# Two of four graph layers computed over lists of edges instead of over the full mask

## The chip, the cores and the metric

The kernel runs on one core of one Trainium2 chip. The metric is the time of one execution in device microseconds (us), first to last instruction of that core. Engines are named as in the profile: PE is the matrix engine and PEld its weight loads, DVE the vector engine, ACT the scalar engine, POOL GpSimd, SP the engine whose queue issues most DMAs.

## The reference, cut to what matters

The input `x` is 16 batches of 1024 nodes with 256 features; `adj` is one symmetric 1024x1024 mask for all of them. Four layers follow one another, each of the form `x = x + attention(relu(layernorm(x)))`:

```python
# layers 0 and 3: 4 heads of 64 features     (layer 1: the same with 1 head of 256)
Wh = (h @ W).reshape(B, N, 4, 64)
e  = s_src[:, :, None, :] + s_dst[:, None, :, :]        # one score per (query, neighbour, head)
e  = leaky_relu(e, 0.2);  e = where(adj, e, -inf)
out = elu(einsum('bijh,bjhd->bihd', softmax(e, axis=2), Wh))
# layer 2: e = (h W1)(h W2)^T, same mask and softmax, values h W3, relu
```

The mask is the same in every batch and layer. With this case's data it has 9052 ones among 1,048,576 places: 8.8 neighbours a query on the mean, 19 at most, at most 7 within any 128 neighbours in a row. Of 32 queries in a row the neighbours number 255 to 316.

## The kernel before, in words

`fast` (the other function, `general`, runs only where a check on the inputs fails) writes its whole program out through a planner. `Plan.add` takes a step: its engine, an assumed cost, a due time, the steps it waits for, and the buffers that it takes and gives back (`bufs`, by tag). `Plan.order` plays the steps through with those costs, always the ready step with the earliest due time on each engine, and the instructions are emitted in that order. Each engine then runs its own list strictly in that order on the chip. Layers of different batches are thereby woven into one another: constants such as `PERIOD`, `START`, `LEAD`, `LATER` say at which multiple of a period each (batch, layer) is due.

Nothing is gathered: every layer works on all 1024x1024 pairs of a batch, in two halves of 512 queries and 8 tiles of 128 neighbours. Scores of layers 0, 1, 3 factor, so that a weight is `max(row[query], ke[neighbour]) * mask`.

- `Layer.prologue` normalises (statistics by DVE at L831/L832, `rstd` by POOL's `pow` at L867, `h` by ACT at L901), transposes `h` with DMAs (L928, from SP), projects (`projected`, PE), and evicts the values into `val`, each head with one more column for the denominator (L982 to L993). The query factors are turned by PE (`er`), written to DRAM (L1062) and read back spread over 128 partitions (`row`, L1075, 256 KB each).
- `steps_a` serves layers 0 and 3. For each half, head and neighbour tile, 64 steps a layer: one DVE instruction writes a 128x512 tile `p` of weights (`weigh`, L1128), then PE multiplies it in (`attend`: for each of 4 query tiles `product` with 65 columns of `val`, gathered in a PSUM tile `acc`). Afterwards `invert` (L1161), `divide` (L1172 on DVE or L1175 on ACT), `elu` (L1094 to L1108) and, after layer 3, the store (L1199).
- `steps_b` serves layers 1 and 2, with `accb` as accumulator: 64 products a query tile, 257 columns wide. Layer 2 also computes its scores on PE (`pp<-qT,hT`).

`product` (L584) splits the stationary operand into two tiles of 64 columns which write to the two halves of the partitions; each call of `matmul` on f32 stands in the trace as two MATMULs and two LDWEIGHTS. So a layer 0 or 3 has 64 steps x 4 query tiles x 2 = 512 calls.

The order of DMAs on SP is that of the list too: a `row` load whose buffer isn't free holds up the transposes behind it.

Of the kernel before, what the change touches and what calls it, by code (L numbers as in the profile page):

```python
# [9 lines left out]
F32 = mybir.dt.float32  # L10
BF16 = mybir.dt.bfloat16
I32 = mybir.dt.int32
U16 = mybir.dt.uint16
# [36 lines left out]


PERIOD, EARLY = 190.0, 0.8711
START = {0: 0.0, 1: 1.0292, 2: 2.3297, 3: 3.7503}
LEAD = {0: 0.5727, 1: 0.718, 2: 0.2478, 3: 2.1041}
STEP = {0: 0.0094, 1: 0.0707, 2: 0.069, 3: 0.055}
WHEN = {
    (1, "weights"): ((-0.4736, 0.0028), (-0.1245, 0.0433)),
    (1, "attended"): ((0.7291, 0.0065), (0.2632, 0.174)),
    (2, "weights"): ((-0.1558, 0.0082), (0.3907, 0.0165)),
    (2, "attended"): ((0.6931, 0.1127), (0.5021, 0.0038)),  # L60
# [7 lines left out]
}  # L68
AHEAD = {
# [11 lines left out]
class Plan:  # L81
# [9 lines left out]
    def __init__(self, free, strict):  # L91
        self.free, self.steps, self.wide = dict(free), [], set()
        self.queues = {tag: [] for tag in strict}

    def add(self, engine, cost, due, fn, after=(), take=(), give=(), wide=False):
        s = len(self.steps)
        if wide:
            self.wide.add(s)
        self.steps.append([engine, cost, due, fn, tuple(a for a in after if a is not None), take, give])
        for tag in set(take) & set(self.queues):  # L100
            self.queues[tag].append(s)
        return s

    def order(self):
# [13 lines left out]
        self.starts = {}  # L118
# [10 lines left out]
        while True:  # L129
            again = True  # L130
            while again:
                again = False
                for engine, queue in ready.items():
# [19 lines left out]
                    k = pick[1]  # L153
                    for tag in steps[k][5]:
                        free[tag] -= 1
# [11 lines left out]
            if what == 0:  # L167
                idle[steps[k][0]] = True
            else:
                for tag in steps[k][6]:  # L170
                    free[tag] += 1
# [7 lines left out]
        return [steps[k][3] for k in res]  # L179
# [362 lines left out]
def fast(  # L542
# [26 lines left out]
    plan = Plan(bufs, ("p", "p1", "acc", "accb", "val4", "val1", "x", "row4", "row1"))  # L569
# [4 lines left out]
    dram = ctx.enter_context(tc.tile_pool(name="dram", bufs=4, space=DRAM))  # L574
    psum = ctx.enter_context(tc.tile_pool(name="psum", bufs=1, space=PSUM))

    def buf(tag, shape, dtype=F32, name=None):
        pool = psum if tag in ("pp", "acc", "accb") else sb
        return pool.tile(shape, dtype, name=name or tag, tag=tag, bufs=bufs[tag])
# [35 lines left out]
    faults = const.tile([P, 2], F32, name="faults")  # L615
    fine = const.tile([1, 1], F32, name="fine")
    x_tiles, mean_var, early = {}, {}, []
# [12 lines left out]
    def load_x(b, due, after=()):  # L630

        res = []
        for n, (t0, t1) in enumerate(PARTS[b == 0]):
# [3 lines left out]
            def fn(its=slice(t0, t1), apart=apart):  # L637
                if its.start == 0:
                    x_tiles[b] = buf("x", [P, NT, F], name="xt")
                (nc.scalar if apart else nc.sync).dma_start(  # L640
                    out=x_tiles[b][:, its, :], in_=x[b].rearrange("(t p) f -> p t f", p=P)[:, its, :]
                )

            s = plan.add(ACT if apart else SP, 0.5, due, fn, after, take=() if t0 else ("x",))
            after = () if b == 0 else (s,)
            res += [landed(s, due, 128 * (t1 - t0))] * (t1 - t0)
# [82 lines left out]
    def mask_steps():  # L729
        done = {}  # L730
        for n, (half, jh) in enumerate(((0, 0), (0, 1), (1, 0), (1, 1))):
            due, quarter = 15.0 + n if half else -1.5 if jh else SOON - 5.2, {}

            def load(half=half, jh=jh, quarter=quarter):
                raw = quarter["raw"] = buf("x", [P, HT, HALF], I32, name="raw")
                rows = adj[half * HALF : (half + 1) * HALF, jh * HALF : (jh + 1) * HALF]
                nc.sync.dma_start(out=raw, in_=rows.rearrange("(t p) j -> p t j", p=P))


            loaded = landed(plan.add(SP, 0.9, due, load, (first_x[2 if n == 0 else -1],), take=("x",)), due, 1024)  # L740
            for t in range(HT):
                tiles = {}

                def positive(t=t, tiles=tiles, quarter=quarter):
                    tiles["pos"] = sb.tile([P, HALF], BF16, name="pos", tag="h", bufs=bufs["h"])
                    nc.vector.tensor_scalar(tiles["pos"], quarter["raw"][:, t, :], 0.0, None, op0=OP.is_gt)

                s = plan.add(DVE, 0.36, due, positive, (loaded,), take=("h",), give=("x",) if t == HT - 1 else ())
# [8 lines left out]
                def keep(tiles=tiles, half=half, jh=jh, t=t):  # L757
                    copy = nc.scalar.copy if half else nc.vector.tensor_copy
                    copy(mask[half][jh][:, :, t * P : (t + 1) * P], tiles["tp"])

                s = plan.add(*((ACT, 0.6) if half else (DVE, 0.65)), due, keep, (s,), give=("pp",))
# [12 lines left out]
    def w12_steps(due):  # L774
# [28 lines left out]
        for fc in range(KC):  # L803
# [12 lines left out]
            s = plan.add(PE, 0.9, due, multiply, tuple(last), take=("pp",), give=("p1",), wide=True)  # L816
# [7 lines left out]
    def statistics(b, t, due, after):  # L824


        def fn():
            if b not in mean_var:
                mean_var[b] = small.tile([P, NT, 2], F32, name="mv", bufs=6)
            st = small.tile([P, 6], F32, name="bn")  # L830
            nc.vector.bn_stats(st, x_tiles[b][:, t, :])  # L831
# [5 lines left out]
    class Layer:  # L837
        def __init__(self, b, layer):
            self.b, self.layer = b, layer
            self.heads, self.gat = LAYERS[layer]  # L840
            self.closed = []

            self.filling = layer == 0 or layer == 3 and b >= B - 2

        def prologue(self, due, step, stats, direct=False):
# [7 lines left out]
            tag = f"val{heads}"  # L853
            T = {}
# [3 lines left out]
            for n, its in enumerate(slice(*part) for part in parts):  # L858

                def norm(its=its, n=n):  # L860
                    if n == 0:
                        T["rstd"] = small.tile([P, NT], F32, name="rstd")
                        T["shift"] = small.tile([P, NT], F32, name="nshift")
# [5 lines left out]
                def norm3(its=its, n=n):  # L869
# [7 lines left out]
                    self.val = buf(tag, [P, NT, heads, d + 1], name="val")  # L877
                    if self.gat:
                        ke = self.factors = small.tile([P, COLS], F32, name="ke", tag=f"ke{heads}", bufs=2)
# [3 lines left out]
                    else:  # L883
                        nc.gpsimd.memset(self.val[:, :, :, d : d + 1], 1.0)
                        self.hT = sb.tile([P, KC, N], F32, name="hT")
                        self.qT = sb.tile([P, KC, N], F32, name="qT")
# [4 lines left out]
                take = () if n else (tag,) if self.gat else (tag, "hq")  # L891
# [3 lines left out]
            for n, t0 in enumerate(range(0, NT, 2)):  # L895
                at = due + n * step

                def normed(t0=t0):
                    for t in (t0, t0 + 1):
# [3 lines left out]
                            x_tiles[b][:, t, :],  # L903
# [5 lines left out]
                s = plan.add(ACT, 1.05, at, normed, (ready[t0],), take=("h", "h"))  # L909
# [45 lines left out]
                for k in range(2):  # L955
                    t = t0 + k

                    def projected(t=t, t0=t0, k=k):
                        pv = T["pv", t] = buf("pp", [P, HALF])
# [9 lines left out]
                    s2 = plan.add(  # L969
                        PE, 0.9, at + (k + 1) * step / 3, projected, (s, w_ready), take=("pp",),  # L970
# [3 lines left out]
                    def evict(t=t, many=heads > 1 and (direct or not self.filling)):  # L974
                        to = self.val[:, t, :, :d]
# [4 lines left out]
                        a = self.val[:, t, :, d : d + 1]  # L980
# [4 lines left out]
                        nc.scalar.activation(self.ke[:, :, t], T["pv", t][:, F:cols], AF.Exp)  # L985
# [3 lines left out]
                    def scaled(t=t):  # L989
                        to = self.val[:, t, :, :d]  # L990
                        of = T["pv", t][:, :F].rearrange("p (h d) -> p h d", h=heads)
                        a = self.val[:, t, :, d : d + 1]
# [4 lines left out]
                    s2 = plan.add(ACT, cost, at, evict, (s2,), give=() if many else ("pp",))  # L997
# [3 lines left out]
                    evicted.append(s2)  # L1001
            at = due + 4 * step
            self.ready, self.queries = evicted, ([], [])
            if not self.gat:
                for dc in range(KC):
                    for n0 in range(0, N, HALF):

                        def query(dc=dc, n0=n0):
                            pq = T["pq", dc, n0] = buf("pp", [P, HALF])
# [9 lines left out]
                        s = plan.add(PE, 1.72, at, query, (*copies, *w12_ready), take=("pp",))  # L1019

                        def keep(dc=dc, n0=n0):
                            nc.scalar.copy(self.qT[:, dc, n0 : n0 + HALF], T["pq", dc, n0])
# [3 lines left out]
            self.rows, self.row_ready = {}, {}  # L1026

            if direct:
                for half in range(2):
                    for hd in range(heads):  # L1030

                        def spread(half=half, hd=hd):
# [453 lines left out]
```

## Time and profile before

| | |
|---|---|
| runs before | 2969.36 and 2970.18 us, median 2969.77 |
| profiled execution: span | 2969.3 us |
| PE busy | 2915.6 us, 98% |
| DVE busy | 2644.8 us, 89% |
| ACT busy | 1920.6 us, 65% |
| POOL busy | 227.0 us, 8% |
| DMA | 188.06 MB, mean 63 GB/s |
| granted PE clock, mean | 0.996 |

The table is read row against row: the time of an engine can't be less than its busy time, and only PE's comes near the span. "Busy" on PE is the union of overlapping instructions, so a group's busy time divided by its number of calls is the pace at which calls leave, while "mean ns" is the duration of a single one.

### The profile page before, as it was taken

How to read it: one execution, taken by the hardware profiler on the slowest of the kernel's cores; microseconds unless marked ns; L12 is line 12 of the kernel's file. 1: busy time of each engine (PE TensorE's matmuls, PEld its weight loads, DVE VectorE, ACT ScalarE, POOL GpSimd, SP SyncE). 2: the span in 40 equal slices, each digit the busy share in tenths (PEclk: the TensorE clock that was granted, in tenths of full speed). 3: DMA queues.
4: the chain of work that ended last, by engine and by line, in shares of the span. 5: the costliest groups of instructions: out<-in, count | busy, mean ns of one | idle time of the engine just before them, and what ended most of it. 6: DMA issues, size and time to landing. Idle time of an engine off the chain costs nothing.

```text
span 2969.3 us, 108633 instructions
## 1 busy us (share of the span) xinstructions
PE 2915.6 (98%) x47954; PEld 2296.6 (77%) x47954; DVE 2644.8 (89%) x5284; ACT 1920.6 (65%) x4776; POOL 227.0 (8%) x153
## 2 busy tenths in 40 slices
PE   8799999999999999999999999999999999999997
PEld 6687968778787786777787777887977779787876
DVE  8998988789989898998989989889999989687788
ACT  6785776876665767565775656766675575664633
POOL 2110100100100001010000100001001000000000
PEclk9999999999999999999999999999999999999999
DMA  4331323323122342322323213231332333120310
GB/s 144 71 86 39 67 51 94 74 60 81 42 59 66 66 80 52 79 46 56 77 70 78 45 50 73 66 69 47 71 75 51 63 76 70 34 59 23 63 34 25
DMA packets 344048, 188.06 MB, mean 63 GB/s; under 512 B 268880, under 2 KB 304400, under 8 KB 343568
## 3 DMA queue, kind: packets, MB, share of 16 engines
q1 hardware_dynamic: 342880, 180.25, 26.9%
q8 instruction: 378, 6.19, 0.9%
q14 instruction: 102, 0.84, 0.1%
q10 hardware_dynamic: 688, 0.79, 0.1%
HBM read 98.63 MB, written 17.33 MB: 39 GB/s over the span
## 4 chain that ended last, share of the span: by engine, by line
PE 85%; DVE 11%; ACT 2%; issue 1%; DMA 0%; POOL 0%; DVEq 0%; POOLq 0%
PE pp L584 30%; PE acc L584 27%; PE accb L584 27%; DVE p L1128 6%; DVE o L1099 1%; DVE bn L831 1%; DVE p L1252 0%; DVE p L1251 0%; DVE mv L832 0%; DMA turned<-planes 0%; DVE xt L1101 0%; ACT hTp L942 0%; ACT h L901 0%; DVE p L1219 0%; ACT planes L924 0%
## 5 line engine op out<-in xcount | busy, mean ns | idle before, releaser
L1128 DVE SCALAR_TENSOR_TENSOR p<-row,ke,mask 128x512 f32<-128x512 f32 x2048 | 1456.9, 766 | 63.5 <-PE acc L584 62.7
L584 PEld LDWEIGHTS acc<-val,p 128*64 128x64 f32 x32768 | 1066.3, 139 | 112.2 <-DVE p L1128 37.1
L584 PE MATMUL acc<-val,p 128*64 128x65 f32 x32768 | 1072.6, 223 | 29.9 <-DVE p L1128 28.6
L584 PE MATMUL accb<-val,p 128*64 128x257 f32 x8192 | 925.8, 380 | 0.1
L584 PEld LDWEIGHTS accb<-val,p 128*64 128x64 f32 x8192 | 703.3, 137 | 163.1 <-issue 5.1
L584 PE MATMUL pp<-qT,hT 128*64 128x512 f32 x2048 | 462.1, 593 | 0.2 <-ACT val L982 0.2
L584 PE MATMUL pp<-w,hTp 128*64 128x264 f32 (+1 forms) x3072 | 385.3, 388 | 4.8 <-ACT hTp L942 4.8
L584 PEld LDWEIGHTS pp<-qT,hT 128*64 128x64 f32 x2048 | 176.5, 137 | 208.2 <-issue 203.1
L584 PEld LDWEIGHTS pp<-w,hTp 128*64 128x64 f32 x3072 | 248.8, 138 | 87.9 <-issue 18.3
L901 ACT ACTIVATE h<-xt,nshift,rstd 128x256 f32<-128x256 f32 x512 | 275.1, 597 | 57.1 <-DVE nshift L870 56.5
L1286 ACT ACTIVATE o<-accb,rdens 128x256 f32<-128x256 f32 x128 | 60.7, 474 | 345.7 <-DVE rdens L1278 333.5
L924 ACT COPY planes<-h 128x512 uint16<-128x512 uint16 x496 | 281.2, 621 | 3.3 <-DMA turned<-planes 3.3
L1251 DVE SCALAR_TENSOR_TENSOR p<-u,p 128x512 f32<-128x512 f32 x256 | 174.9, 683 | 74.0 <-ACT p L1247 73.7
L867 POOL TENSOR_TENSOR rstd<-rstd,neg_half 128x8 f32<-128x8 f32 (+2 forms) x67 | 120.2, 1794 | 1425.6 <-DVE rstd L864 1029.0
L1246 ACT ACTIVATE u<-pp 128x512 f32<-128x512 f32 x256 | 153.0, 598 | 109.7 <-PE pp L584 100.5
L1175 ACT ACTIVATE o<-acc,rden 128x64 f32<-128x64 f32 x572 | 131.9, 317 | 140.7 <-DVE rden L1161 118.1
L831 DVE BATCH_NORM_STATS2 bn<-xt 128x6 f32<-128x256 f32 x512 | 212.0, 414 | 11.2 <-DMA xt<-in_x_dram 3.3
L942 ACT COPY hTp<-turned 128x1024 uint16<-128x1024 uint16 x184 | 214.0, 1167 | 6.8 <-DMA turned<-planes 6.7
L1252 DVE TENSOR_TENSOR p<-p,mask 128x512 f32<-128x512 f32 x256 | 177.1, 692 | 8.8
L1219 DVE SCALAR_TENSOR_TENSOR p<-row,ke,mask 128x512 f32<-128x512 f32 x256 | 182.1, 748 | 0.0
L987 ACT ACTIVATE val<-pp,val 128x64 f32<-128x64 f32 (+1 forms) x640 | 179.4, 347 | 0.0
L1247 ACT ACTIVATE p<-pp,shift_col 128x512 f32<-128x512 f32 x256 | 176.0, 687 | 0.0
(87 smaller groups left out, 1839.0 us busy)
## 6 DMA issues: line engine op xcount, KB each, us to landing
row<-er_d SPq DMA_DIRECT2D x272, 256.0 KB
xt<-in_x_dram SPq DMA_DIRECT2D x31, 512.0 KB
out_dram<-xt SPq DMA_DIRECT2D x31, 512.0 KB
raw<-in_adj_dram SPq DMA_DIRECT2D x4, 1024.0 KB
raw<-in_adj_dram SPq DMA_DIRECT2D x16, 256.0 KB
turned<-planes SPq DMA_TRANSPOSE x248
w<-in_L_gnn_W_dram SPq DMA_DIRECT2D x2, 256.0 KB
wraw<-in_L_gnn_W_dram SPq DMA_DIRECT2D x2, 256.0 KB
```

Of the source, the lines that this page charges most:

```text
L584: nc.tensor.matmul(to[c : c + COLS], stationary[:, c : c + COLS], moving, start=start, stop=stop, skip_group_check=True,)
L831: nc.vector.bn_stats(st, x_tiles[b][:, t, :])
L901: nc.scalar.activation(h, x_tiles[b][:, t, :], AF.Relu, bias=T["shift"][:, t : t + 1], scale=T["rstd"][:, t : t + 1],)
L924: nc.scalar.copy(to[:, :, :, k, :], of)
L942: nc.scalar.copy(bits, T["tp", t0].rearrange("p s c q -> p c q s"))
L987: nc.scalar.mul(to[:, hd, :], of[:, hd, :], a[:, hd, :])
L1128: nc.vector.scalar_tensor_tensor(p, lay.rows[half, hd], lay.ke[:, lay.heads + hd, jt : jt + 1], mask_of(half, jt), op0=OP.max, op1=OP.mult)
L1219: nc.vector.scalar_tensor_tensor(p, lay.rows[half, 0], lay.ke[:, 1, jt : jt + 1], mask_of(half, jt), op0=OP.max, op1=OP.mult)
L1246: nc.scalar.activation(u, e, AF.Exp, scale=1.0 - SLOPE)
L1247: nc.scalar.activation(p, e, AF.Exp, bias=shift_col, scale=SLOPE)
L1251: nc.vector.scalar_tensor_tensor(p, u, 1.0, p, op0=OP.max, op1=OP.mult)
L1252: nc.vector.tensor_mul(p, p, mask_of(half, jt))
```

## The change

Of the 32 (batch, layer) pairs of layers 0 and 3, all but (0, 0) and (15, 3) leave `steps_a`. They are joined in 15 slots of two. A slot's members share one table in DRAM and one stream of gathers:

```python
GROUP, TILES, MOST_OF = 32, 3, 24
WIDTH = 264
SLOTS = (((1, 0), (2, 0)), ((3, 0), (0, 3)), ((4, 0), (5, 0)),
         *(((b, 0), (b - 5, 3)) for b in range(6, 16)),
         ((11, 3), (12, 3)), ((13, 3), (14, 3)))
```

**Lists, once** (`edge_steps`, due early). For each group of 32 queries the neighbours are listed, padded to 3 tiles of 128 places: 32 groups x 3 = 96 lists. Eight loads of 512 KB bring the mask; for each, DVE runs a 128x1024 multiply, eight `max` over 128 columns (eight largest each), three `max` over 64 and two `match_replace`; then ranks, one-hot matrices and products choose what stands at each place. Left behind are `edge_of` (row numbers, 4096 and more at empty places), `pick` (which query of 32 an edge belongs to, 0 or 1) and its transpose `picked`. POOL clears the gather buffers once. A third check joins the two that decide whether `general` must run (a query with 24 neighbours, a group with over 384, or 8 within 128).

**Prologue of a member.** The values, 4x65 columns, and the neighbours' factors, 4 columns, make up a row of 264 f32 that goes to the table (`store`, SP, 264 KB for two tiles). The query factors aren't read back as `row`: DVE writes them in three bf16 parts, PE multiplies them by `picked` into one factor per edge (24 products of 128x48 a member, bf16), DVE adds the parts (`rs`).

**The slot** (`steps_c`), 24 units of four lists:

```python
        for u in range(UNITS):                      # UNITS = 8 query tiles x 3
            for g in range(NG):                     # NG = 4 groups of 32 queries
                nc.gpsimd.indirect_dma_start(
                    out=T["vg", u][:, g, :], out_offset=None, in_=slot.table[:, :],
                    in_offset=bass.IndirectOffsetOnAxis(ap=edge_of[:, u * NG + g : u * NG + g + 1], axis=0),
                    bounds_check=N - 1, oob_is_err=False,
                )
...
                nc.vector.tensor_tensor(w, slot.rs[...], vg[:, :, :, heads * (d + 1) :], OP.max)
                nc.vector.tensor_tensor(p, pick[:, u, :]..., w..., OP.mult)
...
                for m in range(many):               # two members
                    for hd in range(heads):
                        for g in range(NG):
                            nc.tensor.matmul(
                                acc[g * GROUP : (g + 1) * GROUP, hd, :],
                                p[:, m * heads + hd, g * GROUP : (g + 1) * GROUP],
                                vg[:, g, lo : lo + d + 1],
                                start=kt == 0 and hd == 0, stop=kt == TILES - 1, skip_group_check=True,
                            )
```

A gather fetches 128 rows of 528 f32 (2112 bytes) by the row numbers. `w` has 32 elements a partition, `p` 1024. The stationary tiles are 32 columns wide and write to four quarters of the partitions.

**Close of a query tile** (`closing`): reciprocal and one multiply of 128x256 on DVE, `elu` for two tiles at once. POOL's additions (L1108) and ACT's divisions and multiplications for these layers go to DVE.

**Buffers and queues.** `bufs` is cut anew; `Plan.homes` names each buffer by number:

```diff
-        "x": 5, "val4": 2, "val1": 2, "hq": 1, "row4": 3, "row1": 2, "h": 4, "planes": 2, "turned": 2, "hTp": 2, "p": 8, "p1": 18,
-        "u": 2, "o": 1, "ex4": 1, "o1": 2, "ex1": 2, "pp": 4, "acc": 2, "accb": 2,
+        "x": 14, "xp": 4, "xr": 2, "vs": 5, "dense": 1, "val1": 2, "hT": 1, "qT": 1, "row": 2, "h": 4, "planes": 2, "turned": 2, "hTp": 2, "p": 2,
+        "p1": 12, "u": 2, "o1": 2, "ex1": 1, "vg": 3, "rs": 2, "parts": 2, "pp": 3, "acc": 3, "accb": 2,
```

`x` is no longer kept from layer to layer across an edged layer: it is loaded again before a layer 0 closes, and before layer 3 it is written to DRAM (`kept`) and read back (60 DMAs of 256 KB of each kind). The 240 `row` loads and 30 `er_d` stores of the members go. All constants of the order (`PERIOD`, `START`, `LEAD`, `WHEN`, `LATER`, `AHEAD`, `SLOT`) get new values, so that the order of nearly all instructions changes. Layers 1 and 2 and the two pairs left in `steps_a` compute as before.

Instructions emitted: 11,520 calls of the 32-column product take the place of 15,360 of the 16,384 that wrote `acc`; 1440 gathers stand on POOL; DVE has 360 `w` and 360 `p` in place of 1920 of its 2048 L1128. In PE's list neighbours with stationary tiles of unlike width meet some 735 times, before 50 times.

More of the change, by code (lines that the diff above doesn't have):

```diff
@@ L47 @@
 TURNED_ON_PE = ((0, 0), (15, 3))
[L52 to L55, printed above, removed]
+GROUP, TILES, MOST_OF = 32, 3, 24
+WIDTH = 264
+SLOTS = (
+    ((1, 0), (2, 0)),
+    ((3, 0), (0, 3)),
+    ((4, 0), (5, 0)),
+    *(((b, 0), (b - 5, 3)) for b in range(6, 16)),
+    ((11, 3), (12, 3)),
+    ((13, 3), (14, 3)),
+)
+SLOT_AT = {members: 1.0 + n for n, members in enumerate(SLOTS)}
+EDGED = {member: members for members in SLOTS for member in members}
+BASE = [SLOT_AT[EDGED[b, 0]] if (b, 0) in EDGED else -0.6 for b in range(16)]
+SLOT = {
+    'span': 0.717, 'at': -0.009, 'gather': 0.165, 'begin': 1.751, 'load': 0.715, 'close': 0.781,
+    'edges': 39.716, 'fill': -1.263, 'weigh': 0.198, 'attend': 0.313, 'rows': -0.018, 'again': 1.292,
+    'once': 0.886, 'pace': 8.614,
+}
+SLOT_LATER = {
[4 rows of a table added]
+}
+PERIOD, EARLY = 164.109, 0.908
+START = {0: 0.0, 1: 1.025, 2: 2.028, 3: 3.1}
+LEAD = {0: 1.356, 1: 0.086, 2: 0.817, 3: 0.019}
+STEP = {0: 0.0612, 1: 0, 2: 0.041, 3: 0}
 WHEN = {
[L57 to L60, printed above, removed]
+    (1, 'weights'): ((0.07, 0.1144), (0.727, 0)),
+    (1, 'attended'): ((0.181, 0.0663), (0.606, 0.0919)),
+    (2, 'weights'): ((0.01, 0.0389), (0.459, 0.0217)),
+    (2, 'attended'): ((0.418, 0.0608), (0.7, 0.0785)),
 }
 LATER = {
[4 rows of a table removed]
[7 rows of a table added]
 }
 AHEAD = {
[5 rows of a table removed]
[7 rows of a table added]
 }
@@ L814, in multiply @@
                     )
-            s = plan.add(PE, 0.9, due, multiply, tuple(last), take=("pp",), give=("p1",), wide=True)
+            s = done = plan.add(
+                PE, 0.9, due, multiply, (*last, done if fc else None), take=("pp",), give=("p1", "p1") if fc else (), wide=True
+            )
             res.append(
@@ L840, in __init__ @@
             self.heads, self.gat = LAYERS[layer]
-            self.closed = []
-            self.filling = layer == 0 or layer == 3 and b >= B - 2
+            self.closed, self.spilled = [], {}
+            self.filling = False
+            self.slot = slots[EDGED[b, layer]] if (b, layer) in EDGED else None
+            self.member = EDGED[b, layer].index((b, layer)) if self.slot else 0
         def prologue(self, due, step, stats, direct=False):
@@ new lines, in steps_a, with store @@
+            for k in range(half * HT, (half + 1) * HT, 2):
+                its = (k, k + 2)
+                s2 = lay.elu(T, k, its, at - early[0], (s,), (1, 1.25, 1.3), (0, F), ("o1",))
+                if lay.layer == 3:
+                    def store(its=its, b=lay.b):
+                        nc.sync.dma_start(
+                            out=out[b].rearrange("(t p) f -> p t f", p=P)[:, its[0] : its[1], :],
+                            in_=x_tiles[b, its[0] // 2],
+                        )
+                    landed(plan.add(SP, 0.5, at, store, (s2,)), at, 256, give=(("x", x_home[lay.b, k // 2]),))
@@ L1390, in say @@
             nc.vector.tensor_scalar(flag, fine, 1.0, None, op0=OP.is_lt)
-        s = plan.add(DVE, 0.8, due, compare, (*after, *fine_ready))
+        s = plan.add(DVE, 0.8, due, compare, (*after, *fine_ready), take=("u",), give=("u",))
         s = plan.add(PE, 0.4, due, total, (s,), take=("pp",))
@@ L1428, in fast @@
     check_denominators((B + 2) * PERIOD, tuple(lays[B - 1, 2].closed))
-    for fn in plan.order():
-        fn()
+    order = plan.order()
+    plan.homes()
+    for plan.now in order:
+        plan.steps[plan.now][3]()
 def tile_gnn_stack(tc: tile.TileContext, *args: bass.AP):
```

688 lines of the change are left out of this document (577 added, 111 removed), and 27 rows, old and new, of tables (AHEAD, LATER, SLOT_LATER).

## The prediction

> **What bounds the kernel now.** I read the busy totals first, then the chain that ended last, then the groups, then stretches and single moments. Totals and chain:
>
> ```profile
> PE 2915.6 (98%) x47954; PEld 2296.6 (77%) x47954; DVE 2644.8 (89%) x5284; ACT 1920.6 (65%) x4776; POOL 227.0 (8%) x153
> ...
> PE 85%; DVE 11%; ACT 2%; issue 1%; DMA 0%; POOL 0%; DVEq 0%; POOLq 0%
> ```
>
> The span is 2969.3 us; PE is idle for 2969.3 − 2915.6 = 53.7 us of it, and the chain runs through PE for 85%. PE is the bound, DVE follows at 89%, POOL is all but free. The groups say what PE spends its time on, and what the change takes from DVE and POOL:
>
> ```profile
> L1128 DVE SCALAR_TENSOR_TENSOR p<-row,ke,mask 128x512 f32<-128x512 f32 x2048 | 1456.9, 766 | 63.5 <-PE acc L584 62.7
> ...
> L584 PE MATMUL acc<-val,p 128*64 128x65 f32 x32768 | 1072.6, 223 | 29.9 <-DVE p L1128 28.6
> ...
> L584 PE MATMUL accb<-val,p 128*64 128x257 f32 x8192 | 925.8, 380 | 0.1
> ...
> L584 PE MATMUL pp<-qT,hT 128*64 128x512 f32 x2048 | 462.1, 593 | 0.2 <-ACT val L982 0.2
> ```
>
> Layers 0 and 3 hold 1072.6 us of PE (L584, `acc`) and 1456.9 us of DVE (L1128): the change strikes the largest item of both. Pace of PE where nothing holds it up, and cost of a turn to the full width:
>
> ```profile
> 192.05 7.17 PE L584 MATMUL acc<-val,p 128*64 128x65 f32 x240
> ```
>
> ```profile
> 2934.40 0.41 PEld L1036 LDWEIGHTS pp<-ident,ke 128*128 128x128 f32 x4
> 2934.98 2.00 PEld L584 LDWEIGHTS acc<-val,p 128*64 128x64 f32 x64 [0.17 <-issue]
> ```
>
> 240 MATMULs in 7.17 us is 29.9 ns each, 59.8 ns a call (two MATMULs), 119.6 ns for two calls side by side. After the full-width transposes the weight loads pause 0.17 us with nothing to wait for. POOL, in groups by form:
>
> ```profile
> L867 POOL TENSOR_TENSOR rstd<-rstd,neg_half 128x8 f32<-128x8 f32 x62 | 115.4, 1862 | 1400.6 <-DVE rstd L864 1004.0 <-DVE rden L1161 370.2 <-DMA turned<-planes 16.4
> L1108 POOL TENSOR_TENSOR xt<-xt,o 128x1024 f32<-128x1024 f32 x35 | 93.2, 2664 | 1042.6 <-DVE o L1099 783.2 <-DVE rden L1278 122.0 <-ACT hTp L942 49.4
> L689 POOL TENSOR_TENSOR wa<-w,a_bc 128x256 f32<-128x256 f32 x10 | 10.2, 1041 | 18.9 <-issue 12.8 <-ACT junk_a L709 3.2 <-DVE a_bc L679 2.8
> ```
>
> One instruction of POOL costs 1 to 2.7 us whatever its size. That becomes the question.
>
> **The change part by part.** The sum is made on the profiled execution, 2969.3 us, 0.5 below the median of 2969.77.
>
> *PE, removed.* 30 of 32 layers leave L584 `acc`: 30/32 × 1072.6 = 1005.6 us. With them go 60 of the 92 `er` transposes (12.6 us in all): 8.2.
>
> *PE, products of the lists.* 11,520 calls of 65 columns, four side by side. How long two side by side must stream follows from two rows: `accb`, 257 columns, 925.8/4096 = 226 ns a call, 452 a pair; `qT`, 512 columns, 462.1/1024 = 451 ns, 902 a pair; 1.765 ns a column, hence 115 ns for 65, of 119.6 measured. Today's pace is thus that of the data, not of the instructions, and 64 columns of weights a load become 32. Best case: four in 119.6 ns, 29.9 a call, 344 us. Worst: calls leave no faster than now, 59.8, 689 us. Only the issue of four instructions a call does not shrink, and it accounts for 5 of 119.6 ns today, so I take a value nearer the lower end: 40 ns, 461 us. The Trainium skill, "TensorE: Matmul & The Clock Gate", section "Wait — 56ns, not 53.3ns?", speaks against that: starts never come closer than about 25 ns however few the columns, by which 23,040 MATMULs would be an estimated 576 us, 115 more; no row here shows starts closer than 29.9 ns, so the rule is untested by this trace.
>
> *PE, other additions.* 720 spreads of 128x48 with a 128-column load: 64-column bf16 loads with their product come every 31 ns in the trace (8 in 0.39 us, 16 in 0.64), twice the columns 62 ns, 45 us; the slowest like row, f32 transposes at 109 ns an instruction, gives 78. I take 60. List building (48 transposes, 48 selections, 8 spreads): 9. Width turns: some 690 more, 0 to 0.17 us each, so 0 to 117; the row is for full width and the turns here are between 32 and 64, so I take half, 0.08, 55 us.
>
> PE busy: 2915.6 − 1005.6 − 8.2 + 461 + 60 + 9 + 55 = 2487 us.
>
> *DVE.* Gone: 30/32 × 1456.9 = 1365.8. New: 360 units, `w` at 0.19 us (rows of few elements take 0.15 to 0.18) and `p` of 1024 elements at the 1.225 us that L1101 takes at 128x1024: 509. Factors per edge: 30 × 1.6 (six of 128 elements at 0.29, the shortest fewer) = 48, and 90 additions of 384 elements at about 0.5 = 45. Values of layer 0 (L993 twice as often): 54. Divisions that ACT did: 58. `elu` additions that POOL did and the smaller tiles: 70. Lists, once: about 67. Sum 2644.8 − 1365.8 + 851 = 2130 us, below PE by 350. The cover for all of it is PE; were PE at 2130, DVE would be the bound.
>
> *ACT* loses 540 divisions of 317 ns and 512 multiplications of 315, and gains 240 short ones of 0.185 and smaller `elu` tiles: some 1770 us, no bound.
>
> *POOL.* Today 227, less 93 of L1108, leaves 134; plus 1440 gathers. No row shows one. From below a memset, 0.10 us; from above L1108, 2.66. A gather has one index a partition and 128 rows to describe, so it is no memset; nearest are the 1.04 of L689 and the 1.86 of L867, and I take their middle, 1.45: 2088 us. Gathers can only start when the lists stand. That is after about 130 us: the mask loads and 67 us of DVE work, in turn with the 45 us of (0, 0)'s own weights. POOL's other work after that is some 120, and after the last gather some 40 us of closing remain. POOL's path: 130 + 2088 + 120 + 40 = 2378, below PE by 230 with its idle time; it is hidden while a gather costs under 1.61. The Trainium skill, "DMA: Bandwidth & Descriptors", section "Anatomy of one DMA — SWDGE (gpsimd) path", gives a fixed cost of about 2.0 us for such a DMA, mostly waiting for the receipt; if POOL itself were held that long, the estimate for its path would be 3170, and the change a loss; no row of this trace has a DMA of POOL to show it.
>
> *What waits behind the gathers.* POOL's list is in order: `rstd` (L867, 62 times) stands behind whole runs of gathers, and a gather waits for one of three `vg` buffers, which PE's product gives back. A late product so delays a `rstd`, and with it a prologue and PE's next projection. A unit has 3 × 4 × 1.45 = 17.4 us for its round of gathering 5.8, landing about 3, `weigh` 1.4 and products 1.3, so 6 us are left for waiting in DVE's and PE's lists.
>
> *SP and DMA.* 240 row loads (61 MB) and their waits go: SP stood 896.4 us behind L1128 for `row`. New are 120 table stores, 60 reloads of `x`, 60 stores and 60 reloads of `kept` (79 MB), and 15 × 9052 × 2112 bytes = 287 MB of gathers: 188 − 61 + 79 + 287 = 493 MB, 189 GB/s over 2605 us. The first 50 us of the trace moved 181 GB/s at a DMA share of 0.56, so the engines have room; landings may lengthen, and the cover is that loads are due well ahead.
>
> *Idle time of PE.* Today's 53.7 stays. At the start PE has batch 0 alone (its four layers but the last: about 150 us of PE) and a few projections, some 200 us, until the first slot is gathered at 130 + 96 × 1.45 = 269; with part of that slot done on the way, 45 idle. At the end the last two slots bring 60 us of products for 280 us of gathers, with (14, 2), (15, 1), (15, 2) and (15, 3) to fill in: 20. Together 65.
>
> Sum: 2487 + 53.7 + 65 = 2605 us, 0.877 of before.
>
> **The rivals.**
>
> *The gathers become the bound.* Path: 290 + 1440 × g. At g = 1.61 it meets 2605, at 1.86, which L867 costs, it is 2968: no gain; at 2.1, 3314. For it: POOL's `pow` takes 1.64 us in its quiet runs and 1.94 to 2.08 in others, beside DVE, and DVE stays 82% busy; 0.4 more on 1.45 is already 1.85. Against: L689's 1.04. This one ends on the other side from g = 1.86; the chain of buffers above works the same way, as it adds to each unit.
>
> *PE's issue is the limit.* 689 us in place of 461: 2605 + 228 = 2833. For it: no row shows MATMULs closer than 29.9 ns. Against: 115 of 119.6 ns are explained by data.
>
> *It does not take place.* The checks could send the whole through `general`. Against: 19 neighbours against 23 allowed, 316 against 384, and 7 against 7. I leave it out.
>
> **How the numbers follow.** PE bound as summed: 0.52, own range 2480 (products at 344 us and no turns: 2605 − 172, with somewhat more idle) to 2740 (turns at 117, spreads at 78, 55 more idle). PE's issue: 0.12, 2833. Gathers bound: 0.36; of it 0.08 ends under 2910 (g to 1.82), 0.08 between 2910 and 3029, 0.20 above. A measurement of this kernel can tell about 2% from no change. Faster: 0.52 + 0.12 + 0.08 = 0.72; same 0.08; slower 0.20. The range is 2480 to 3050 (g = 1.92), which leaves out 0.05 below and 0.15 above.
>
> **What would show it.** Right: PE again over 93% busy, `acc<-vg,p` at 400 to 520 us, L1128's successor at 180, POOL 80 to 90% busy with gaps before gathers that end on PE (the buffers). Wrong: POOL over 95% between the first and last gather and PE idle before `acc` with DVE `p` as the releaser, above all with a gather over 1.6 us; or the 32-column calls near 60 ns; or DVE's `p` far over 1.23 us because POOL works beside it.

## The result and the profile after

In the runs that the prediction is held against, the changed kernel took 3401.77 us (two runs, 3399.82 and 3403.71) against 2969.77: a ratio of 1.145, 95% interval 1.142 to 1.148. It was slower, where 2605 and faster had been forecast. The page of that run (span 3402.0 us), totals and groups:

```profile
PE 2862.6 (84%) x41039; PEld 1703.3 (50%) x41039; DVE 2140.9 (63%) x4945; ACT 1733.5 (51%) x4067; POOL 1751.6 (51%) x1570
```

```profile
L1718 POOL DMA_INDIRECT vg<-table,edge_of x1440 | 1610.8, 1119 | 1121.6 <-PE acc L1764 646.7
```

DVE (2141) and ACT (1734) came out as forecast. PE is busy for 2863 us and idle for 539, of which the prediction had 119. POOL, the rival's bound, is busy for half of the span, and its longest wait is for PE, not PE's for it. What PE waits for, in total, times and longest:

```profile
PE acc L1764 <- issue: 267.9, 613, 4.5
PE acc L1764 <- DVE p L1742: 55.3, 32, 6.7
PE pp L666 <- ACT hTp L1310: 42.2, 11, 23.5
```

"issue" is a pause for which the profile shows no wait at all. The profile of before has no such row for PE's products; here they are the largest by far (309 us over all lines). PE's timeline at one such moment (start, length, instructions, idle time before):

```profile
1803.89 1.13 PE L1764 MATMUL acc<-vg,p 128*32 128x65 f32 x64
...
1814.92 0.81 PE L1764 MATMUL acc<-vg,p 128*32 128x65 f32 x33
1816.15 0.32 PE L1764 MATMUL acc<-vg,p 128*32 128x65 f32 x3 [0.41 <-issue]
1816.92 0.32 PE L1764 MATMUL acc<-vg,p 128*32 128x65 f32 x4 [0.45 <-issue]
1817.65 0.32 PE L1764 MATMUL acc<-vg,p 128*32 128x65 f32 x5 [0.41 <-issue]
1818.38 0.31 PE L1764 MATMUL acc<-vg,p 128*32 128x65 f32 x4 [0.41 <-issue]
```

A block of 64 such MATMULs took 1.13 us at 1803.89; the one that starts at 1814.92 soon begins to trickle: three to five, then 0.41 to 0.45 us of nothing, one round every 0.73 to 0.77 us. Their weights `p` had been there since 1806.4. By stretches (PE busy is the second number, then PEld, DVE, ACT, POOL, the granted clock, DMA share, GB/s), first before, then after:

```profile
0.00:300.00 300.00, 269.75 (x4555) 210.44 (x4557) 273.34 (x558) 207.49 (x596) 44.06 (x39) 0.98 0.32 84
300.00:2700.00 2400.00, 2391.66 (x38916) 1880.72 (x38914) 2146.59 (x4310) 1591.83 (x3887) 168.23 (x107) 1.00 0.29 64
```

```profile
0.00:300.00 300.00, 183.41 (x2923) 128.35 (x2924) 232.14 (x620) 139.45 (x399) 102.47 (x105) 0.83 0.51 142
300.00:2700.00 2400.00, 2087.80 (x29206) 1229.18 (x29207) 1488.13 (x3431) 1303.62 (x3045) 1294.75 (x1150) 0.94 0.60 151
```

PE loses 86 us in the first 300, and 304 in the next 2400, where it also runs at a granted clock of 0.94 instead of 1.00. So the two questions were: what makes PE trickle, and what costs the rest.

### The profile page after: what moved, and what is told of

Same layout as the page of the kernel before. It is cut to its first block, busy times and chain, and to the rows that moved or that the text cites. A ratio compares the mean times of both kernels' runs of the same rounds, so it can differ in the third digit from the quotient of the medians.

```text
span 3402.0 us, 98157 instructions
## 1 busy us (share of the span) xinstructions
PE 2862.6 (84%) x41039; PEld 1703.3 (50%) x41039; DVE 2140.9 (63%) x4945; ACT 1733.5 (51%) x4067; POOL 1751.6 (51%) x1570
## 5 line engine op out<-in xcount | busy, mean ns | idle before, releaser
L1718 POOL DMA_INDIRECT vg<-table,edge_of x1440 | 1610.8, 1119 | 1121.6 <-PE acc L1764 646.7
L666 PE MATMUL accb<-val,p 128*64 128x257 f32 x8192 | 999.7, 392 | 36.8 <-issue 15.2
L1764 PE MATMUL acc<-vg,p 128*32 128x65 f32 x23040 | 615.0, 228 | 329.9 <-issue 267.9
L666 PEld LDWEIGHTS accb<-val,p 128*64 128x64 f32 x8192 | 627.4, 140 | 375.3 <-issue 101.9
L1764 PEld LDWEIGHTS acc<-vg,p 128*32 128x32 f32 x23040 | 444.2, 113 | 610.1 <-issue 472.7
L666 PE MATMUL pp<-w,hTp 128*64 128x264 f32 (+1 forms) x3072 | 435.6, 422 | 69.5 <-ACT hTp L1310 42.2
L1742 DVE TENSOR_TENSOR p<-pick,w 128x1024 f32<-128x1024 uint8 x360 | 441.6, 1227 | 18.7 <-PE acc L1764 2.1
L1544 ACT ACTIVATE ex<-o 128x512 f32<-128x512 f32 (+1 forms) x256 | 134.3, 524 | 215.2 <-DVE o L1579 120.4
L1549 DVE SCALAR_TENSOR_TENSOR o<-ex,o 128x512 f32<-128x512 f32 (+1 forms) x256 | 141.0, 551 | 75.8 <-ACT ex L1545 66.9
L1793 DVE SCALAR_TENSOR_TENSOR p<-row,ke,mask 128x512 f32<-128x512 f32 x256 | 178.2, 743 | 6.4 <-DMA row<-er_d 6.4
```

Source lines behind the costliest of these rows:

```text
L666: nc.tensor.matmul(to[c : c + COLS], stationary[:, c : c + COLS], moving, start=start, stop=stop, skip_group_check=True,)
L1718: nc.gpsimd.indirect_dma_start(out=T["vg", u][:, g, :], out_offset=None, in_=slot.table[:, :], in_offset=bass.IndirectOffsetOnAxis(ap=edge ...
L1742: nc.vector.tensor_tensor(p.rearrange("p m (g q) -> p m g q", g=NG), pick[:, u, :].rearrange("p (g q) -> p g q", g=NG).unsqueeze(1).to_bro ...
L1764: nc.tensor.matmul(acc[g * GROUP : (g + 1) * GROUP, hd, :], p[:, m * heads + hd, g * GROUP : (g + 1) * GROUP], vg[:, g, lo : lo + d + 1], ...
L1793: nc.vector.scalar_tensor_tensor(p, lay.rows[half, 0], lay.ke[:, 1, jt : jt + 1], mask_of(half, jt), op0=OP.max, op1=OP.mult)
```

## The experiments

The runs were made in six sessions, each on one chip; I name the chips A (first session), B, C, D (two sessions) and E. Where the expectations say "call", they mean such a session. The chip of the recorded runs is not known. "Pauses" are the sums of PE's MATMUL rows with "issue" as the cause (309 us in the changed kernel, none in the kernel before). Where an edit changes the values of the output, the expectation or the text says so; in these kernels the switch to `general` is turned off too (`fine < 1` becomes `fine < -1`).

**First session, chip A: is it the traffic, or how densely the calls follow?** Narrow gathers, in the changed kernel (the products read a constant, so the output changes, and the stores to the table shrink as the rows do):

```diff
-  out=T["vg", u][:, g, :],              # 528 columns
+  out=T["vg", u][:, g, : 4 * many],     # 8 columns; table [N, 8]
-  vg[:, g, lo : lo + d + 1],
+  still.unsqueeze(1).to_broadcast([P, 5, 13]),   # + one call on vg where kt > 0
```

> The changed kernel with as many gathers (1440, 128 indices each) that bring 32 bytes an edge instead of 2112: only the factors. The products of the lists keep their number, order and width but stream a constant in place of the gathered values; one call more in two of three units still reads what was gathered. The output is so not the reference's. Theory S (the gathers' traffic slows the supply of PE's instructions): the idle time of PE with nothing to wait for (about 250 us in gaps over 250 ns in the changed kernel) all but goes, the clock returns towards 0.99, 2600 to 2800 us. Theory I (32-column calls outrun the supply of instructions whatever else runs): the gaps stay, 3300 to 3400. Theory P (the pace of POOL, one gather every 1.3 us in a ring of three buffers): next to no change, over 3250.

Measured: 3956 us, pauses 491 us. It lies far above the ranges of theories S and I, and theory P's "next to no change" does not fit either: with a 66th of the bytes it is 555 us slower than the recorded run. What held of theory I is that the pauses stay.

Gathers added to the kernel before, with rows of 2048 and of 32 bytes (`%d` is 512 or 8):

```diff
+  nc.gpsimd.indirect_dma_start(out=buf("gx", [P, 512])[:, :%d], out_offset=None, in_=rows_of,
+      in_offset=IndirectOffsetOnAxis(ap=edge_of[:, 0:1], axis=0), bounds_check=95 * 61, oob_is_err=False)
-  "p": 8,
+  "p": 6, "gx": 2,
```

> The kernel before with 1440 gathers on POOL added, 45 in each layer 0 and 3, each 95 rows of 2048 bytes into a buffer that nothing reads (280 MB in all; two buffers of p fewer, for room). All else as before, 64-column calls. S: PE shows gaps with nothing to wait for, as in the changed kernel, and the time rises by 100 us or more over the same with short rows. I: no such gaps, under 50 us over the same with short rows. P: no gaps; any rise is as large with short rows.

> The control to the run with wide rows: the same 1440 gathers added to the kernel before, 32 bytes a row in place of 2048. All three theories: no gaps of PE with nothing to wait for. S and I: within 60 us of the kernel before (2970 to 3030); P: POOL's order costs something, the same rise as with wide rows.

Measured: 3661 and 3925 us; both end in a tail in which POOL gathers on, 99% of PE's instructions being done by 3120 and 3492. Pauses 44 and 429 us. So the pauses can be had in the old kernel too, with 64-column calls: density alone is not the cause. And wide rows bring the fewer of them, so bytes are not it either. What PE waits for in the second:

```profile
PE acc L585 <- issue: 398.9, 584, 3.2
PE acc L585 <- DVE p L1134: 34.7, 35, 2.4
```

Half the density in the changed kernel (130 columns, so the values of the output change):

```diff
-  vg[:, g, lo : lo + d + 1],
+  vg[:, g, lo : lo + 2 * (d + 1)],
```

> The changed kernel with 130 columns instead of 65 in each call of the lists' products (same number of calls and weight loads, same gathers; the output is so not the reference's). PE's instructions then come half as densely. I: the gaps with nothing to wait for all but vanish, and the 250 us that go pay for most of the 340 us of longer streams: 3400 to 3520. S: the gaps stay, 3650 to 3750. P: the products are hidden by the gathers' pace, under 3450, with POOL's gaps before a gather shorter.

Measured: 3485 us, pauses 210 us. The time lies in the range of theory I, but the pauses, which it let all but vanish, stay for the most part, as theory S said; inconclusive by itself.

**Second session, chip B: is it POOL's work for a gather?** Plain DMAs of 128 rows in sequence in place of each gather, issued by SyncE, then by POOL:

```diff
-  nc.gpsimd.indirect_dma_start(out=T["vg", u][:, g, :], ..., in_=slot.table[:, :], ...)
+  r = P * ((u * NG + g) % NT)
+  nc.sync.dma_start(out=T["vg", u][:, g, :], in_=slot.table[r : r + P, :])     # or nc.gpsimd
```

> The first runs fell against both first theories: the kernel before shows 89 gaps over 250 ns of PE with nothing to wait for beside wide gathers and 611 beside narrow ones, and the changed kernel 983 with narrow gathers against 598. So bytes are not the cause, and density alone is not. New theory G: POOL's own work for a gather (indices into descriptors, 128 a gather) disturbs the supply of PE's instructions, the more the closer the gathers follow each other. Rival T: any DMA into the buffers of the values does it. Here the changed kernel with each gather replaced by a plain DMA of 128 rows in sequence from the same table, issued by SyncE (389 MB in place of 287; the values are other rows, so the output is not the reference's). G: the gaps all but vanish, clock near 0.99, 2750 to 2950. T: as many gaps or more, 3400 or over.

> As the run with plain DMAs, but issued from POOL's list, in the order of the changed kernel (389 MB, output not the reference's). If the profile puts these on a queue of hardware descriptors: as the run from SyncE for G (2750 to 2950), 3400 or over for T. If POOL makes the descriptors itself, G expects gaps again.

And in the kernel before, gathers that move no row (`base=0` becomes `base=100000` in the list of places), and iotas in place of gathers:

> The kernel before with 1440 gathers as in the run with narrow rows, but every index is out of bounds, so that no row moves. G: gaps of PE with nothing to wait for as with narrow rows (hundreds of us). T: none, within 60 us of the kernel before until POOL's tail.

> The kernel before with POOL occupied at the same places for about the same time (2880 iota instructions of 128x512, about 0.55 us each) and no DMA. G and T: no gaps with nothing to wait for, 2970 to 3030; if gaps come here too, it is POOL's being busy and not the gather.

Measured, in this order: 3053, 3115, 3405 (PE's instructions 99% done by 2987, then POOL's tail) and 3016 us; pauses 20, 10, 0 and 0 us. The first two times lie in no theory's range. With every index out of bounds POOL works as long on a gather, and there are no pauses; so at this point it looked as if rows that an indirect DMA really moves were needed. None of these four kernels was run on chip A, though, so what they show holds for chip B alone.

**Third session, chip C: which rows?** Indices in sequence; plain narrow DMAs from POOL; rows of 2048 bytes:

```diff
-  in_offset=IndirectOffsetOnAxis(ap=edge_of[:, u * NG + g : u * NG + g + 1], axis=0)
+  in_offset=IndirectOffsetOnAxis(ap=seq[:, (u * NG + g) % NT : (u * NG + g) % NT + 1], axis=0)
```

> Theory G as put last fell too: with every index out of bounds POOL works as long on each gather and PE shows no gap over 250 ns without a wait; with plain DMAs, from SyncE or from POOL, of more bytes into the same buffers, PE shows 10 and 5. So it needs rows that an indirect DMA really moves. Here the changed kernel with the same indirect DMAs, but the indices are 128 rows in sequence, all in bounds (389 MB, the same rows as in the runs with plain DMAs; output not the reference's). Theory D (the indirect form with rows to move is enough, wherever the rows lie): over 400 gaps, 3350 or more. Theory A (it is the rows' addresses: repeated and scattered rows): gaps all but gone, about the 3115 of the plain DMAs from POOL.

```diff
-  nc.gpsimd.indirect_dma_start(out=T["vg", u][:, g, : 4 * many], ...)
+  nc.gpsimd.dma_start(out=T["vg", u][:, g, : 4 * many], in_=slot.table[r : r + P, :])
```

> Plain DMAs from POOL of 128 rows of 32 bytes, the products stream a constant as in the run with narrow gathers (output not the reference's). Theory D and theory A: no gaps, below the 3115 of the run with wide plain DMAs (its transposes came late under 389 MB), 2950 to 3080. Theory Z (small pieces written into SBUF are what stalls PE, whoever describes them): several hundred gaps, 3500 or more.

```diff
-  out=T["vg", u][:, g, :],
+  out=T["vg", u][:, g, :512],           # table [N, 512]
```

> The changed kernel with rows of 2048 bytes in place of 2112, so four whole pieces of 512 and no remainder of 64 (the last head of the second layer and its factors read the first layer's; output not the reference's). Theory Z (the remainder): gaps fall below 100 as with 2048-byte rows beside the kernel before, 3050 to 3200. Theories D and A: as the changed kernel, 3350 to 3420.

Measured: 3001, 2796 and 2949 us, each below what any of the theories gave; pauses 5, 1 and 6 us. The last looked like an answer: shorten the rows by 64 bytes and the pauses go. But apart from the recorded run all kernels with pauses had run on A, and all on B and C were all but without (20 us at most). So the next session ran the changed kernel as it is.

**Fourth session, chip D: kernel or chip?**

> The changed kernel as it is, a second time. The kernels with many gaps of PE without a wait (narrow and wide gathers, products of 130 columns) were all run on one chip and those without gaps on others, so that the gaps may belong to the chip and not to the kernels. Theory C (the gaps come and go with the chip): here a time other than 3402, near 3000 if this chip is of the kind without gaps, with under 20 gaps over 250 ns; or, if it is of the other kind, near 3402 together with gaps in the run with rows of 2048 bytes. Theory Z (rows of 2112 bytes with indices out of bounds among them make the gaps): 3390 to 3410 with about 600 gaps.

> The changed kernel with rows of 2048 bytes, a second time (the last head of the second layer and its factors read the first layer's; output not the reference's). Theory Z: 2949 within 15 whatever the chip. Theory C: within 60 of whatever the changed kernel takes in this call.

> The kernel before with 1440 gathers of rows of 32 bytes added, a second time. Theory Z: again over 500 gaps and 3925 within 60. Theory C: gaps here only if the changed kernel has them in this call; without them PE's work is done by about 3000 and the rest is POOL's tail, 3400 to 3700.

Measured: the changed kernel 2964.0 us (median of 8, 2954.9 to 2976.5), 0.998 of before (0.996 to 1.000); rows of 2048 bytes 2952.9, 0.996 (0.990 to 1.001); the kernel before with narrow gathers 3406 (99% of PE by 2987). Pauses 8, 6 and 0 us. The rows of 2048 bytes fit both theories; the other two fit theory C alone. The last is the kernel that took 3925 on A; here its waits read:

```profile
PE acc L585 <- DVE p L1134: 38.6, 37, 2.5
PE pp L922 <- ACT h L907: 9.4, 2, 8.2
PE pp L585 <- ACT hTp L948: 6.5, 6, 2.6
```

Same program, 429 us of pauses there and none here: they go with the chip (or with something that stays the same throughout a session). With that, the grounds for the theories of remainders, addresses and indirect rows are gone, as these compared kernels on A with kernels on other chips. What in a gather brings the pauses on A is open: there only indirect DMAs that move rows were run, and the narrow ones brought more pauses than the wide ones.

**Fifth session, chip D again: the rest.** The kernel with narrow gathers again (its edit is the first above), and the changed kernel without its first slot:

> The kernel with gathers of 32 bytes an edge and products of a constant (output not the reference's), a second time, on another chip. On a chip without the gaps it splits what plain narrow DMAs gained (2796 against 2964 for the changed kernel): if it was the bytes and their landing, 2790 to 2830 here as well; if it was POOL's pace (1.14 us a gather and 0.26 between, against 0.54), 2900 to 2970. On a chip with the gaps, over 3800.

```diff
 SLOTS = (
-    ((1, 0), (2, 0)),
     ((3, 0), (0, 3)),
```

> The changed kernel without its first slot: layer 0 of samples 1 and 2 goes the way of the kernel before, so that PE has work while the lists are built (one buffer of x fewer, for room; their places in the plan are mine and not tuned). Start theory: PE's busy time in the first 300 us rises from 186 by 40 to 80, against some 30 us more products, so 2910 to 2960 on a chip without the gaps. Rival (the chain of gathers from slot to slot sets the end): one slot of 15 less, 2850 or below. Rival (the room in the first 300 us is only moved on): 2960 to 3020.

Measured: 2849 us with pauses of 1 (3956 on A), between its two forecasts and nearer to that of the bytes; and 3183 (1.073, 1.066 to 1.081) with 8, above all three forecasts. In the second, PE's first 300 us hold 207 us of work in place of 186, but the first gather starts at 490.8 us in place of 181.4 and the last at 3112.8. I take it that the room at the start was only moved on and that the order of the plan was worse, which is not shown. That says little of the start itself.

**Sixth session, chip E: a third look, and half the bytes.**

> The changed kernel as it is, a third time, for the chip: 2950 to 2980 with no more than some gaps of PE without a wait, or near 3402 with about 600 of them; nothing between is expected by theory C.

```diff
-  out=T["vg", u][:, g, :],
+  out=T["vg", u][:, g, :WIDTH],         # table [N, 264]; the second layer's rows go to a spare table
```

> The changed kernel with gathers of 264 columns in place of 528, one layer's values for both (as many gathers; output not the reference's). On a chip without the gaps: if the rows' bytes cost what the narrow gathers left (2964 less 2849), about half of it goes, 2890 to 2920; if bytes matter only above what the landing hides, under 2870; if they do not matter, 2950 to 2970.

Measured: 2962.9 us (0.9975, 0.9950 to 0.9999), as theory C said, and 2888.7 for the half rows (0.972, 0.970 to 0.975), 1 us below the range in which about half of the narrow gathers' gain comes with half of the bytes; pauses 5 us in both.

Without the pauses, the changed kernel's page (span 2954.8 us; totals, a stretch, PE's waits):

```profile
PE 2572.4 (87%) x41039; PEld 1549.6 (52%) x41039; DVE 2132.6 (72%) x4945; ACT 1729.2 (59%) x4067; POOL 1781.5 (60%) x1570
```

```profile
0.00:300.00 300.00, 189.06 (x3171) 133.18 (x3171) 239.25 (x639) 152.22 (x420) 116.50 (x119) 0.83 0.57 154
300.00:2700.00 2400.00, 2173.13 (x34262) 1280.38 (x34264) 1715.11 (x3928) 1481.73 (x3435) 1551.39 (x1351) 0.97 0.69 174
```

```profile
PE acc L1764 <- DVE p L1742: 159.8, 92, 7.6
PE pp L666 <- ACT hTp L1310: 54.4, 18, 23.5
PE pp L666 <- ACT hT L1310: 23.7, 18, 4.8
```

PE is busy for 87%, and no other engine for more than 72%. The 160 us end on `p`, which DVE makes from `w`; one step further back, DVE's own waits for the gathered rows, for full rows, half rows and rows of 32 bytes:

```profile
DVE w L1736 <- DMA vg<-table,edge_of: 235.2, 117, 7.9
```

```profile
DVE w L1737 <- DMA vg<-table,edge_of: 197.9, 121, 5.9
```

```profile
DVE w L1738 <- DMA vg<-table,edge_of: 124.8, 75, 5.0
```

The times go down with them: 2963, 2889, 2849, and 2796 with plain narrow DMAs. From the start of a gather to its last packet the trace shows a median of 3.65, 2.84, 2.23 and 1.62 us. Of the 167 us between 2963 and 2796, 114 go with the bytes (most of them the gathers', some the table stores', which are narrow too in that kernel) and 53 with the shorter work and landing of a plain DMA; the runs are on E, D and C, and 2849 and 2796 are single runs. That the landing of the rows costs time is thereby shown.

What holds up the rest is not. One candidate is the round of a buffer (gather, land, weigh, multiply, give back), but no kernel with a fourth `vg` buffer was run. POOL's longest waits in the run of 2954.8 us:

```profile
POOL vg L1718 <- issue: 366.7, 1204, 2.0
POOL vg L1718 <- PE acc L1764: 234.7, 65, 19.6
POOL rstd L1225 <- DVE rstd L1222: 203.7, 27, 55.1
```

From its first gather (183 us) to its last (2885) POOL spends 1639 us on gathers and 367 between them without a wait that the profile shows, 2006 of 2702. It waits 235 us for a buffer that PE gives back and 204 at `rstd` for DVE. So one gather after the other takes three quarters of that stretch, the wait for a buffer less than a tenth.

No kernel with the reference's values beat the kernel before by more than the 0.25% of the last session.

## Why the prediction was wrong, point by point

The forecast was 2605. The recorded 3402 is 797 more: PE's idle time is 539 us where the sum had 119, and its busy time 2863 where it had 2487. Some 438 of the 797 go with the chip or session (3402 less 2964): the pauses, a lower clock (0.928 against 0.951 over the span), and stretched groups (the products of the lists are busy for 615 us in place of 423). Against the profile of 2954.8 us, PE is idle for 157 us more and busy for 290 more. Some 359 the forecast would have missed in the sessions on D and E too, where the changed kernel ran as it is. Both parts by its steps, the second on the profile of 2954.8 us:

- **Idle time of PE ("today's 53.7 stays", with 65 more): the step that failed most.** Measured 382 without the pauses, 539 with them. The start costs 111 of 300 us (30 before), where 45 more were allowed. The middle 2400 us hold 227 of idle time, 124 of it before products whose `p` came late, where before had 8 and the forecast nothing new. The "6 us left for waiting" in the round of three buffers was an average; landing was put at "about 3", for which it named no row, and has a median of 3.65 and a tenth of cases over 5.6 us, and POOL stands 204 us at `rstd` for DVE with gathers queued behind.
- **PE busy 2487, measured 2572: near, by misses that set each other off.** The removal was over-counted: 1005.6 is from a group's busy time, which overlaps its neighbours' (the groups of before add up to 3129 us, PE's busy time is 2916). For the same reason busy time divided by calls is not quite the pace, as the section on the profile before had it: 1072.6 us over 32,768 MATMULs are 32.7 ns, the pace is 29.9. By that pace, which the prediction itself had read, 30,720 MATMULs are 918.5, 87 less. Measured against forecast, products and turns took 423 for 516 and spreads 30 for 60; but `accb` took 951 where it had 926, `w,hTp` 409 for 386 and `qT` 471 for 462, at a clock of 0.97 in the middle where it was 1.00. Counted so that each instant belongs to one group only, the removal falls short by 107, what was added costs 142 less, and what was to stay as it was 120 more: together the 85.
- **Products of the lists, 461 with bounds 344 to 689: in an unbroken burst the lower bound was the right one; over the run the group is busy for 423.** Two bursts of the run of 2954.8 us:

```profile
1810.02 1.13 PE L1764 MATMUL acc<-vg,p 128*32 128x65 f32 x64
...
1818.16 2.08 PE L1764 MATMUL acc<-vg,p 128*32 128x65 f32 x128
```

64 more in 0.95 us are 14.8 ns a MATMUL, 29.7 a call. The rule of the Trainium skill, "TensorE: Matmul & The Clock Gate", section "Wait — 56ns, not 53.3ns?", that starts never come closer than about 25 ns, does not hold for calls on 32-column tiles side by side. The prediction called the rule untested; but the 29.9 ns of its row are a mean, and within those 240 MATMULs of the kernel before the starts are by turns 7 and 52 ns apart.
- **POOL's gather 1.45 us: right in size.** 1.14 on average and 0.25 of pause (367 us over 1440), 1.39. "1 to 2.7 us whatever its size" was a misreading, as `rstd` takes 0.71 us at 128x2, 1.13 at 128x4 and 1.86 at 128x8. The rival in which POOL's own time is the bound (2292 us at that price) did not come about as put, though one of its signs did: PE idle before `acc` with DVE `p` as the releaser, 160 us. What the Trainium skill, "DMA: Bandwidth & Descriptors", section "Anatomy of one DMA — SWDGE (gpsimd) path", puts at about 2.0 us is not far from a narrow plain DMA of POOL: 1.62 us from its start to its last packet, 2.4 to its semaphore (medians). POOL isn't held that long (0.54 us there), as the prediction had left open.
- **DVE 2130, ACT 1770, DMA 493 MB:** measured 2133, 1729 and 494.9. "The engines have room" was wrong in effect: at a DMA share of 0.69 in the middle (0.29 before) the landings are later, and halving the gathers' bytes gives 74 us.
- **The pauses** stood in no term and no rival. The trace of before shows none, and it moves nothing by gathers.

What stays open: what is different on chip A. There the kernel before alone takes its usual 2970, and with gathers it pauses, more with narrow rows (429 us) than with wide ones (44), which also came further apart (1.94 against 1.38 us, medians). Five later sessions on four other chips (B, C, E once, D twice) showed at most 20 us of pauses in any kernel. The packets of q8, one of two DMA queues that the page lists as "instruction", take no longer on A (1.07 to 1.09 us on average in the four runs) than on D (1.09 to 1.11), so slower packets there are not the reason. Whether it is the chip or a state that lasts through a session was not told apart, and that the recorded runs fell on such a chip is inferred from the same pattern in their trace.

## What to carry to other kernels

When engine time is taken off a kernel that is 98% busy on one engine, cost the latency of the loop that replaces it (issue, landing, weighing, product, buffer back) with a spread and not a mean: here PE's busy time fell from 2916 to 2572 us and the time stayed, because its idle time rose from 54 to 382, 111 of it in the first 300 us and, over the whole run, 160 before products whose weights came late. Take savings by the pace of the stream, not by a group's busy time, which counts overlap. And before a slowdown is explained, run the same kernel again on another chip: pauses for which the profile names no wait led to several theories about rows and descriptors that one repeat put aside.

## What the runs showed of the hardware

- On 32-column tiles, four side by side, a MATMUL of 65 columns starts every 14.8 ns on the mean, against 29.9 on 64-column tiles, two side by side: 29.7 ns a call (two MATMULs) against 59.8.
- An indirect DMA of 128 indices holds POOL for 1.01 us (median) and the next follows 0.30 us later (median); as many rows by a plain DMA from POOL hold it for 0.54 us. With every index out of bounds it is held as long (1.13 on average).
- Gathers beside the kernel before cost PE little where there are no pauses: 99% of its instructions done by 2987 us with 32-byte rows, against 2937 without; POOL's tail then ends at 3404.
- On chip A and in the recorded run PE at times gets a few MATMULs (mostly 3 to 5) every 0.73 us or so with nothing to wait for. All four kernels run on A with a profile had gathers; the kernel before took its usual 2970 there. Two of the four were repeated, on D, and showed 0 and 1 us of such pauses.
